# A selective scan's decays issued up to seven units ahead instead of four

## The chip, the cores and the metric

The program runs on one core of a Trainium2 chip. The core has five engines that work side by side: TensorE (PE in the profile, with PEld its weight loads), VectorE (DVE), ScalarE (ACT), GpSimd (POOL) and SyncE (SP), which here issues the DMAs. Each engine takes its instructions strictly in the order in which they were written, and stands still at the first one whose inputs are not there. The metric is the device time of the whole program in microseconds, the median of several runs.

## The reference

The input is 64 images of 96 channels and 28 by 28 pixels. Four layers follow one another:

- layer 0, a convolution block: 1x1 expansion to 576 channels, SiLU, a 5x5 depthwise convolution whose taps are mixed per image, SiLU, a gate, 1x1 projection, residual;
- layer 1, a state-space block: layer norm, projection to 192 channels and a gate `z`, a 3x3 depthwise convolution, SiLU, and then the selective scan in four directions, with 16 states a channel; output norm, gate, projection, and an MLP with GELU;
- layers 2 and 3: layer norm, a Fourier mixing along the 784 positions, and a feed-forward part whose numbers are rounded to 8-bit floats.

What matters here is the scan. Cut from the reference:

```python
dt = jax.nn.softplus(dt)
A = -jnp.exp(A_logs)

def step(hst, inp):
    dt_t, x_t, B_t, C_t = inp
    dA = jnp.exp(dt_t[..., None] * A[None])
    dBx = dt_t[..., None] * B_t[:, :, None, :] * x_t[..., None]
    hst = hst * dA + dBx
    y_t = jnp.einsum('bkdn,bkn->bkd', hst, C_t)
    return (hst, y_t)
```

`dA` is called the decay below. Softplus needs Exp and Ln; the other layers need SiLU and GELU, and those functions lie in other tables of ScalarE than Exp and Ln.

## The kernel before

**Units.** The images go through in 32 pairs. For one pair the scan is cut into 12 blocks (four directions `k`, three tiles `T` of channels), each block into 16 units `n`. A unit is one tile of 128 rows (32 channels by 4 states) and 784 positions. With `j = n % 4` the unit takes the `j`-th group of 32 channels, and with `g = n // 4` the `g`-th group of four states. So the four units of a group share one `pb` (the B row, spread by TensorE into PSUM), and the four groups of a block share the same four tiles of `dt` and of `u = dt * x`, called `dt4` and `u4`.

One unit (`recur`, `decay` and the loop in `run`):

- ACT, `decay`: `da = Exp(A * dt4)`;
- DVE: `pd = pb * u4` (L1045), then the scan `h` over `da` and `pd` (L1050 or, backwards, L1052);
- POOL: `h = h * cs`, with the C row `cs`;
- PE, `collect`, once in four units: sums over the states into `yp`; `keep` copies `yp` out and SP stores it.

**Order.** Nothing is scheduled at run time. `run` walks over all units, one a step, and writes the instructions of each step down in order: the collection of an earlier group, the product and scan of unit `i`, decays of later units, POOL's multiplication for unit `i - 1`, the `pb` of the next group, the loads. `prepare_block` loads the next block's `dt4` and `u4` from DRAM, one tile at each of the steps that the tuples in it name (`at` is `n` of the current block); `fetch_c` loads `cs`.

**Streams.** Between the steps two streams of other work are written: stream `a` (`first_half`) does layer 0 and the front of layer 1 for the next pair, and stream `b` (`second_half`) the rest of the previous pair. Each has one PSUM bank, `bank_a` or `bank_b`: PE fills it, ACT or DVE empties it, and PE waits for that before the next piece. How many pieces stand between two steps is decided by a small planner, `Clocks`, which adds up assumed durations, an ACT table load of 1.28 among them (`activation`), and by how late a stream is. What is left of a stream at the end of a pair is written before the next pair. Stream `a` also writes the `dt` and `u` of the next pair to DRAM (`product`).

**Decays.** `AHEAD = 4`. The decays of the first four units stand before the scan. At step `i`, when the table that ACT holds is Exp's (`act.current == EXP_LN`), or when fewer than four units are decayed, everything up to unit `i + 4` is decayed. Otherwise, with SiLU's or GELU's table in place, the step goes without; the next step then forces the table back, with two decays behind it. The pool `das` has five buffers, so the decay of unit `i + 4` waits until the scan of unit `i - 1` has read its own. The pool `reps` holds five buffers for `dt4` and five for `u4`.

Loads of Exp's table are recorded at line 152 (`preload_act_table_set`), those of the others at line 157.

Of the kernel before, what the change touches and what calls it, by code (L numbers as in the profile page):

```python
# [35 lines left out]
F32 = mybir.dt.float32  # L36
# [10 lines left out]
L = HW * HW  # L47
# [21 lines left out]
EXP_LN = "natural_log_exp_and_others"  # L69
# [1 line left out]
ROWS5, ROWS3 = 16, 14  # L71
BSLOT = 4 * NF

AHEAD = 4

# [112 lines left out]
class Stream:  # L190
# [10 lines left out]
    def after(self, windows, run):  # L201

        self.later.setdefault(self.window + windows, []).append(run)
# [21 lines left out]
class Model:  # L225
# [3 lines left out]
    def __init__(self, ctx, tc, a, out):  # L229
        self.tc, self.nc, self.a, self.out = tc, tc.nc, a, out  # L230
        self.clocks = Clocks()
        self.alone, self.turn = False, 0
        self.act = Act(tc.nc, self.clocks)
        self.vector, self.gpsimd = Timed(tc.nc.vector, self.clocks.vector), Timed(tc.nc.gpsimd, self.clocks.gpsimd)
        self.npairs = a["x"].shape[0] // 2
        pool = lambda name, bufs, **kw: ctx.enter_context(tc.tile_pool(name=name, bufs=bufs, **kw))
        self.cst = pool("cst", 1)
        self.slots = pool("slots", 1)
        self.small = pool("small", 2)
        self.reps = pool("reps", 5)  # L240
        self.das = pool("das", 5)
        self.hs = deque(self.cst.tile([128, L], F32, name=f"h{i}") for i in range(8))
        self.css, self.bss = pool("css", 3), pool("bss", 2)
        self.rows_a = pool("rows_a", 2)
        self.one = pool("one", 1)
        self.ps1 = pool("ps1", 1, space=PSUM)
        dram = lambda name, bufs: pool(name, bufs, space=bass.MemoryType.DRAM)
        self.dr1, self.dr2, self.dr4 = dram("dr1", 1), dram("dr2", 2), dram("dr4", 4)
        self.setup()
# [270 lines left out]
    def first_half(self, p, st):  # L520
        nc, act = self.nc, self.act
        after = lambda n, run: self.a_stream.after(n, run)
        dma = nc.sync.dma_start
# [7 lines left out]
        for i, k in enumerate((k0, k1)):  # L531
            t = k[:, : 10 * C]
# [37 lines left out]
        pool = self.small.tile([C, 2], F32, name="pool")  # L570
# [108 lines left out]
        for t in range(18):  # L679
            n, h = divmod(t, 2)  # L680
            i = order[n]
# [80 lines left out]
        for b in range(2):  # L762
            for h in range(2):
# [7 lines left out]
                v = xs[b][:, cols(h)]  # L771
# [159 lines left out]
        def product(k, T, dt, x):  # L931
            self.gpsimd.tensor_mul(us[0], dt, x)
            dma(st["dt"][k][T], dt)
            after(1, lambda: dma(st["u"][k][T], us[0]))

        def steps(k):

# [44 lines left out]
    def prepare_block(self, u, at):  # L982

        nc, st, k, T = self.nc, u["st"], u["k"], u["T"]
        if at == 1:
            if u["blk"] in (0, 1, 6, 7):
                self.bs[k] = self.bss.tile([C, L], BF16, name="bsl")
                nc.sync.dma_start(self.bs[k], st["b"][k])
        for name, v, when in (("dt4", "dt", (7, 10, 11, 12)), ("u4", "u", (9, 13, 14, 15))):
            if at in when:  # L990
                j = when.index(at)
                t = self.reps.tile([128, L], F32, name=name)
                self.landed[(u["p"], u["blk"], name, j)] = nc.sync.dma_start(
                    t, st[v][k][T][32 * j : 32 * j + 32, None, :].broadcast_to([32, 4, L])
                )
                self.rep[(u["p"], u["blk"], name, j)] = t
# [87 lines left out]

    def run(self):
        nc, act, clocks = self.nc, self.act, self.clocks
        sts = [dict(p=p) for p in range(self.npairs)]
        self.rep, self.cs, self.bs, self.done, self.stored = {}, {}, {}, None, None
        self.multiplied = self.spread_at = 0.0
        self.past, self.landed = deque(), {}  # L1090
        units = [u for st in sts for u in self.scan_state(st["p"], st)]
        per = len(units) // self.npairs

        fresh = lambda i: 0 < i < len(units) and self.key(units[i]) != self.key(units[i - 1])

        def stream(name, p, start=0):
            pieces = self.first_half if name == "a" else self.second_half
            v = Stream(name, clocks, pieces(p, sts[p]), WINDOWS[name] / (per - 2 - start), start)
            setattr(self, name + "_stream", v)
            return v  # L1100

        def advance(streams, until):


            for v in streams:
                v.begin()
            begins = lambda v: max(clocks.pe, clocks.free["ba"[self.turn] if self.alone else v.name])
            while streams:
                streams = [v for v in streams if begins(v) <= until(v)]
                if streams:  # L1110
                    v = min(streams, key=lambda v: begins(v) - CHOICE * late.get(v, 0))
                    if not v.piece():
                        streams.remove(v)

        late = {}

        def finish(streams):
            while any(not v.over for v in streams):
                advance([v for v in streams if not v.over], lambda v: math.inf)


        first, setup = stream("a", 0), Stream("b", clocks, self.setup_second(), 1, 0)
        while not (first.ready and setup.over):
            advance([v for v in (first, setup) if not v.over and not v.ready], lambda v: math.inf)
            self.alone = setup.over
        first.base, first.rate = first.window, 1
        for at in range(16):
            self.prepare_block(units[0], at)
        self.fetch_c(units[0])
        for u in units[:AHEAD]:  # L1130
            self.decay(u)
        decayed = AHEAD
        clocks.dve = max(clocks.dve, clocks.pe)
        self.spread_b(units[0])
        streams = [first]
        for i in range(len(units) + 6):
            u = units[i] if i < len(units) else None
            n = i % per

            if u and n == 0:  # L1140
                self.alone = i // per in (0, self.npairs - 1)
            if i < per and first.over and streams == [first]:
                streams = [stream("a", 1, n)]
            elif u and n == 0 and i > 0:
                streams = [stream("a", i // per + 1, n)] if i // per + 1 < self.npairs else []
            elif u and n == 6 and i // per > 0:
                streams.append(stream("b", i // per - 1, n))
            if i % 4 == 2 and 6 <= i < len(units) + 3:
                self.collect(units[i - 6 : i - 2])
            if u:  # L1150
                self.recur(u)

                if act.current == EXP_LN or decayed < i + AHEAD:
                    for v in units[decayed : i + AHEAD + 1]:
                        self.decay(v)
                    decayed = i + AHEAD + 1
            if 0 < i <= len(units):
                v = units[i - 1]
                clocks.pool = max(clocks.pool, v["scanned"])
                v["users"] = [self.gpsimd.tensor_mul(v["h"], v["h"], self.cs[self.key(v)])]  # L1160
                v["times_c"] = clocks.pool
            if u:
                if fresh(i + 1):
                    self.spread_b(units[i + 1])
                if i + 16 - u["n"] < len(units):
                    self.prepare_block(units[i + 16 - u["n"]], u["n"])
                if u["k"] == 0 and u["n"] == 8:
                    self.x = self.one.tile([128, L], F32, name="xy")
                    nc.sync.dma_start(self.x, u["st"]["x_in"][u["T"]])
            if i + 3 < len(units) and self.key(units[i + 3]) not in self.cs:  # L1170
                self.fetch_c(units[i + 3])
            if i % 4 == 3 and self.done:
                self.keep()
            elif i % 4 == 0 and self.stored:
                nc.sync.dma_start(*self.stored)
                self.stored = None
            if u:

                late.clear(); late.update({v: v.base + (n + 1 - v.start) * v.rate - v.window for v in streams})
                until = clocks.dve + (EARLY if fresh(i + 2) else ROOM)  # L1180
                due = [v for v in streams if not v.over and (v.open or late[v] > -BEFORE)]
                advance(due, lambda v: until + GAIN * late[v] + max(0, late[v] - (per - n) / 4))
                if n == per - 1:
                    finish(streams)
        finish([stream("b", self.npairs - 1)])
# [512 lines left out]
```

## Time and profile before

| | |
|---|---|
| median of 3 runs | 22,441.52 us (22,433.54 to 22,450.66) |
| profiled execution | 22,503.17 us, span 22,501.5 us |
| mean granted TensorE clock in it | 0.832 of full speed |
| ACT: decays `da` (L157) | 6144, mean 940 ns |
| ACT: table loads | 1124, mean 1283 ns |
| DVE: product (L1045), scan (L1050, L1052) | 6144, mean 979 ns; 6144, mean 1786 ns |
| POOL: `h * cs` (L137) | 6144, mean 1856 ns |
| SP: loads of `dt4`, of `u4` (L993) | 1536 and 1536, 392 KB each |

A row of the profile that names a group gives line, engine, operation, what it writes and reads, the count, then the busy time, the mean of one, and the idle time of the engine just before with what ended it. In a timeline a row gives start, duration, engine, line, operation, tiles and count, and in brackets the idle time before it. A line like L157 or L137 is that of a helper, so groups are told apart by their tiles: `da<-dt` is a decay, `pd<-pb,u` the product, `slot` a buffer of stream `b`, `r`, `k`, `t`, `o` and `pad` buffers of stream `a`. An instruction that waits for several things is put down to one of them, not always to the last.

### The profile page before, as it was taken

The numbers are of one execution on the slowest core, as the hardware profiler recorded it, in microseconds if no ns is written. First come the engines' busy times: TensorE is split into PE (matmuls) and PEld (weight loads), VectorE is DVE, ScalarE is ACT, GpSimd is POOL, SyncE is SP. The second block draws the span as 40 slices with busy tenths as digits, with TensorE's granted clock in tenths as the row PEclk, the third lists the DMA queues.
The fourth block names the chain that finished last, engine by engine and source line by source line (L and its number), as shares of the span: only waits on it lengthen the run. The fifth ranks groups of instructions, "written<-read, shape, count | busy, mean of one in ns | idle before, by whom it ended". The sixth has DMA issues, their size and how long they took to land. (4 is left out here: it accounts for less than half of the span.)

```text
span 22501.5 us, 294265 instructions
## 1 busy us (share of the span) xinstructions
PE 17323.6 (77%) x100890; PEld 6770.9 (30%) x100890; DVE 18393.0 (82%) x15290; ACT 13649.8 (61%) x19357; POOL 15987.8 (71%) x9834
## 2 busy tenths in 40 slices
PE   5778777787777777777877777877778777778766
PEld 2233323332323333323323233323233232333222
DVE  2988888888888888888888888888888888888884
ACT  3566666666666666666666666666666666666654
POOL 2777777777777777777777777777777777777774
PEclk8888888888878888888888888888888888888877
DMA  5766666666666666666666666666666666666642
GB/s 155 229 189 197 201 203 187 191 193 200 202 194 187 189 195 198 205 192 192 192 196 200 193 189 197 196 197 200 193 191 190 195 202 193 193 193 190 199 158 63
DMA packets 1764775, 4285.68 MB, mean 190 GB/s; under 512 B 212500, under 2 KB 447084, under 8 KB 1763177
## 3 DMA queue, kind: packets, MB, share of 16 engines
q1 hardware_dynamic: 1763276, 4266.86, 62.0%
q8 instruction: 799, 13.09, 0.2%
q14 instruction: 700, 5.73, 0.1%
HBM read 3207.28 MB, written 882.92 MB: 182 GB/s over the span
## 5 line engine op out<-in xcount | busy, mean ns | idle before, releaser
L137 POOL TENSOR_TENSOR h<-h,cs 128x784 f32<-128x784 f32 x6144 | 11357.7, 1856 | 3875.7 <-DVE h L1050 1175.6
L1045 DVE TENSOR_TENSOR pd<-pb,u 128x784 f32<-128x784 f32 x6144 | 6016.4, 979 | 2346.6 <-PE pb L253 1029.1
L157 ACT ACTIVATE da<-dt,c_A_logs 128x784 f32<-128x784 f32 x6144 | 5661.2, 940 | 2014.4 <-DVE h L1052 865.4
L1052 DVE TENSOR_TENSOR_SCAN h<-da,pd 128x784 f32<-128x784 f32 x3072 | 5487.5, 1786 | 152.9 <-DVE pd L1045 2.8
L1050 DVE TENSOR_TENSOR_SCAN h<-da,pd 128x784 f32<-128x784 f32 x3072 | 5487.4, 1786 | 130.5
L253 PE MATMUL bank_a<-k,t 128*32 128x392 f32 (+1 forms) x37840 | 3984.7, 529 | 204.3 <-ACT pad L157 122.9
L253 PE MATMUL yp<-h,c_gather 128*32 128x512 f32 (+1 forms) x24576 | 3058.3, 595 | 131.3 <-POOL h L137 121.4
L137 POOL TENSOR_TENSOR slot<-slot,slot 96x392 f32<-96x392 f32 (+6 forms) x1700 | 2203.4, 1301 | 1197.3 <-ACT slot L157 988.8
L157 ACT ACTIVATE slot<-bank_b 128x392 f16<-128x392 f32 (+4 forms) x2546 | 1245.4, 489 | 2277.4 <-PE bank_b L253 2235.4
L253 PE MATMUL pb<-bsl,c_sel 96*128 96x512 bf16 (+1 forms) x4096 | 1192.2, 378 | 1320.4 <-DVE pd L1045 1294.1
L253 PEld LDWEIGHTS bank_a<-k,t 128*32 128x32 f32 (+1 forms) x37840 | 1267.2, 116 | 2391.1 <-issue 1894.3
L253 PEld LDWEIGHTS yp<-h,c_gather 128*32 128x32 f32 x24576 | 797.2, 124 | 2472.3 <-issue 2032.4
L253 PE MATMUL bank_b<-slot,c_center 96*128 96x392 f32 x1736 | 955.3, 638 | 396.1 <-DVE slot L137 243.8
L253 PE MATMUL bank_b<-c_fwd,slot 99*96 99x196 f32 (+1 forms) x3968 | 844.7, 359 | 354.1 <-DVE slot L137 254.9
L253 PEld LDWEIGHTS <-c_sel 96*128 96x128 bf16 x4096 | 353.5, 103 | 2469.8 <-issue 1666.9
L157 ACT ACTIVATE o<-bank_a,bn_b,bn_s 128x392 f32<-128x392 f32 x572 | 385.1, 673 | 1113.1 <-PE bank_a L253 1113.1
L157 ACT ACTIVATE slot<-slot 96x786 f32<-96x786 f32 (+5 forms) x1166 | 890.0, 790 | 85.9 <-DMA slot<-in_dt_w 37.6
L253 PEld LDWEIGHTS bank_b<-c_fwd,slot 99*96 99x96 f32 x3968 | 664.9, 175 | 583.4 <-issue 483.1
L157 ACT ACTIVATE slot<-bank_b,c_l_mix 96x393 f32<-96x393 f32 x736 | 446.1, 638 | 632.5 <-PE bank_b L253 418.0
L137 POOL TENSOR_TENSOR k<-k,r 128x784 f32<-128x784 f32 x256 | 472.0, 1844 | 423.1 <-ACT k L157 276.4
L253 PE MATMUL bank_a<-k,cv_diag 96*32 96x392 f32 x4464 | 612.2, 683 | 207.6 <-DMA k<-padded 175.8
L253 PE MATMUL bank_a<-k,k 108*128 108x392 bf16 x744 | 331.2, 445 | 567.5 <-ACT k L157 203.2
(265 smaller groups left out, 20797.5 us busy)
## 6 DMA issues: line engine op xcount, KB each, us to landing
cs<-crow SPq DMA_DIRECT2D x2048, 392.0 KB
dt<-dt SPq DMA_DIRECT2D x1536, 392.0 KB
u<-u SPq DMA_DIRECT2D x1536, 392.0 KB
k<-padded SPq DMA_DIRECT2D x2304, 256.0 KB
padded<-pad SPq DMA_DIRECT2D x384, 592.0 KB
u<-k SPq DMA_DIRECT2D x384, 392.0 KB
k<-padded SPq DMA_DIRECT2D x576, 224.0 KB
out<-o SPq DMA_DIRECT2D x288, 392.0 KB
```

Source lines behind the costliest of these rows:

```text
L137: return run(out, *args, **kw)
L157: return self.nc.scalar.activation(out, in_, func, **kw)
L253: return self.nc.tensor.matmul(out, weights, moving, **kw)
L1045: self.awaited(nc.vector.tensor_mul(pd[:, :L], self.pb[:, :L], self.rep[(u["p"], u["blk"], "u4", u["j"])]), inputs)
L1050: scan = nc.vector.tensor_tensor_scan(h, da, pd[:, :L], 0.0, ALU.mult, ALU.add)
L1052: scan = nc.vector.tensor_tensor_scan(h[:, ::-1], da[:, ::-1], pd[:, L - 1 :: -1], 0.0, ALU.mult, ALU.add)
```

## The change

- `AHEAD` is 7, and a second mark, `LEAST`, is 3. At step `i`, under Exp's table, at most two units are decayed, and none beyond `i + 7`; under another table nothing is decayed until the reserve has come down to three (`decayed <= i + LEAST`), and then two units are, which brings Exp's table back. So the reserve falls for some steps and is filled by one net unit a step. Seven decays stand before the scan instead of four.
- `das` has eight buffers. `dt4` gets a pool of its own, `dts`, with seven buffers; `reps` keeps `u4` alone.
- `dt4` of the next block is loaded at the steps 5, 7, 9 and 10 instead of 7, 10, 11 and 12; `u4` at the same steps as before. An assertion at build time says that the `dt` or `u` read has been written by then.
- The program is built with `dynamic_dma_scratch_size=1024`; the default of the build is 16384 bytes of each partition. The five further tiles of 784 floats need 15,680 bytes a partition.

```diff
-AHEAD = 4
+AHEAD, LEAST = 7, 3
...
         self.reps = pool("reps", 5)
-        self.das = pool("das", 5)
+        self.dts = pool("dts", 7)
+        self.das = pool("das", AHEAD + 1)
...
         def product(k, T, dt, x):
             self.gpsimd.tensor_mul(us[0], dt, x)
             dma(st["dt"][k][T], dt)
-            after(1, lambda: dma(st["u"][k][T], us[0]))
+            st["made"].add(("dt", k, T))
+
+            def second():
+                dma(st["u"][k][T], us[0])
+                st["made"].add(("u", k, T))
+
+            after(1, second)
...
-        for name, v, when in (("dt4", "dt", (7, 10, 11, 12)), ("u4", "u", (9, 13, 14, 15))):
+        for name, v, when in (("dt4", "dt", (5, 7, 9, 10)), ("u4", "u", (9, 13, 14, 15))):
             if at in when:
                 j = when.index(at)
-                t = self.reps.tile([128, L], F32, name=name)
+                assert u["p"] == 0 or (v, k, T) in st["made"]
+                t = (self.dts if v == "dt" else self.reps).tile([128, L], F32, name=name)
...
-                if act.current == EXP_LN or decayed < i + AHEAD:
-                    for v in units[decayed : i + AHEAD + 1]:
+                if act.current == EXP_LN or decayed <= i + LEAST:
+                    for v in units[decayed : min(decayed + 2, i + AHEAD + 1)]:
                         self.decay(v)
-                    decayed = i + AHEAD + 1
+                        decayed += 1
...
-    nc = bacc.Bacc("TRN2", target_bir_lowering=False, num_devices=1)
+    nc = bacc.Bacc("TRN2", target_bir_lowering=False, num_devices=1, dynamic_dma_scratch_size=1024)
```

More of the change, by code (lines that the diff above doesn't have):

```diff
@@ L1086, in run @@
         nc, act, clocks = self.nc, self.act, self.clocks
-        sts = [dict(p=p) for p in range(self.npairs)]
+        sts = [dict(p=p, made=set()) for p in range(self.npairs)]
         self.rep, self.cs, self.bs, self.done, self.stored = {}, {}, {}, None, None
```

## The prediction

> **What bounds the kernel now.** First the page: the span and the busy row.
>
> ```profile
> span 22501.5 us, 294265 instructions
> PE 17323.6 (77%) x100890; PEld 6770.9 (30%) x100890; DVE 18393.0 (82%) x15290; ACT 13649.8 (61%) x19357; POOL 15987.8 (71%) x9834
> ```
>
> VectorE (DVE) is nearest to the span; ScalarE (ACT), where the change works, is busy 61%. So ACT work counts only where DVE waits for it in the end. Second, twelve windows on one pair of images (pair 15, 10586.6 to 11273.3 us), one per block of 16 units; shown are blocks 0, 9, 10, 11 and the sum. Columns after the window: length, then busy PE, PEld, DVE, ACT, POOL.
>
> ```profile
> 10586.60:10647.40 60.80, 34.46 (x125) 11.98 (x124) 46.43 (x38) 40.24 (x61) 44.91 (x28) 0.64 0.66 232
> ...
> 11071.00:11135.60 64.60, 49.30 (x277) 19.04 (x270) 44.23 (x34) 37.04 (x48) 47.20 (x30) 0.71 0.66 198
> 11135.60:11205.30 69.70, 55.52 (x269) 31.83 (x267) 52.04 (x47) 48.90 (x73) 52.83 (x35) 0.85 0.53 178
> 11205.30:11273.30 68.00, 47.28 (x156) 15.55 (x155) 46.53 (x41) 44.76 (x67) 49.11 (x30) 0.64 0.55 183
> sum 686.70, PE 541.98 PEld 212.59 DVE 573.55 ACT 428.41 POOL 501.24; mean PE 45.16 PEld 17.72 DVE 47.80 ACT 35.70 POOL 41.77
> ```
>
> A step is 686.7 / 192 = 3.58 us. DVE idles 686.7 − 573.55 = 113 us a pair: 20.4 + 17.7 + 21.5 us in blocks 9 to 11, 14.4 in block 0, and some 39 in blocks 1 to 8. Third, what ended DVE's waits before its product, L1045, in total, times:
>
> ```profile
>   PE pb L253: 1029.1, 422
>   ACT slot L157: 415.8, 122
>   ACT xy L157: 221.4, 24
>   ACT r L157: 190.8, 53
>   DMA u<-u: 162.7, 21
> ```
>
> The product reads `pb` and `u4`, not ACT's decays. Pairing each of the 6144 products with its decay by order, the decay had ended a median 10.1 us earlier, and only 13 ended less than 1 us before. No decay is late: more reserve by itself buys nothing. The ACT names are other waits of the same instruction; in both stretches below it is `pb` or `u4` that came last.
>
> **The change part by part.**
>
> *Table loads.* ACT's groups, before:
>
> ```profile
> L152 ACT ACT_TABLE_LOAD x562 | 721.0, 1283 | 10.8 <-PEq L1687 0.7
> L157 ACT ACT_TABLE_LOAD x562 | 721.0, 1283 | 10.1
> ```
>
> The changed program's order has 502 + 530 = 1032 loads for 1124. 92 × 1.283 = 118 us of ACT, 2.9 loads or 3.7 us a pair: less than the marks suggest, since other Exp and Ln work already brings the table back often. [...]
>
> Where it can reach DVE, at unit 16 (ACT's timeline, TensorE's, DVE's):
>
> ```profile
> 10641.23 1.28 ACT L152 ACT_TABLE_LOAD   x1
> 10642.52 1.79 ACT L157 ACTIVATE da<-dt,c_A_logs 128x784 f32<-128x784 f32 x2
> 10644.22 0.33 ACT L157 ACTIVATE r<-bank_a 128x128 f32<-128x128 f32 x2
> ```
> ```profile
> 10644.60 2.85 PE L253 MATMUL bank_a<-k,t 128*128 128x384 f32 x8 [0.91 <-ACT r L157]
> 10647.28 0.50 PE L253 MATMUL pb<-bsl,c_sel 96*128 96x512 bf16 x2
> ```
> ```profile
> 10647.97 0.98 DVE L1045 TENSOR_TENSOR pd<-pb,u 128x784 f32<-128x784 f32 x1 [3.50 <-ACT r L157]
> ```
>
> A forced load and two decays, 3.07 us, stand ahead of the eviction `r`; PE loses 0.91 us, then comes `pb`, and DVE waits 3.50 us. In the changed order this load and both decays follow the evictions. Ends 0 and −3.5 us a pair; I take −0.9, PE's own loss, because PE has 2.85 us of matmuls left before `pb` anyway. The other 1.9 loads a pair (2.4 us) end between 0 and −2.4 us; I take −0.5, near zero, since PE's bank waits hide most of ACT (ACT waited 3302 us for `bank_b`, PE 869 for ACT there).
>
> *Decays earlier, two a step.* A decay seven ahead in 8 buffers needs the scan of the unit before this one, the rule that four ahead in 5 had. So the full reserve stops ACT as before (865.4 + 681.3 us behind L1052 and L1050). By the order 3191 of 5700 decays are issued at seven; the other 44% find free buffers, up to 680 us less ACT waiting. But 1429 steps issue two decays for 523, which holds the evictions behind by 0.94 us each, 42 − 15 = 27 us a pair over evictions that mostly have slack. I cost both at 0; the cover is the reserve of `pb` in blocks 1 to 8, and if it is gone the second is in the rival below.
>
> *dt4 earlier; SP's order.* SP, ACT and DVE around the third block, before:
>
> ```profile
> 10673.66 5.64 SPq L494 DMA_DIRECT2D slot<-slot  x8
> ...
> 10681.13 1.47 SPq L1247 DMA_DIRECT2D slot<-z  x3
> 10682.70 2.80 SPq L506 DMA_DIRECT2D k<-padded  x4
> 10686.26 3.17 SPq L993 DMA_DIRECT2D dt<-dt  x3
> ...
> 10695.28 2.54 SPq L506 DMA_DIRECT2D k<-padded  x4
> 10698.03 0.52 SPq L993 DMA_DIRECT2D u<-u  x1
> ```
> ```profile
> 10697.09 0.95 ACT L157 ACTIVATE da<-dt,c_A_logs 128x784 f32<-128x784 f32 x1 [11.20 <-DMA dt<-dt]
> ```
> ```profile
> 10708.74 0.98 DVE L1045 TENSOR_TENSOR pd<-pb,u 128x784 f32<-128x784 f32 x1 [2.34 <-DMA u<-u]
> ```
>
> ACT stops 11.2 us for unit 33's dt4, 10.8 us after its issue behind a burst; then unit 34's u4, issued behind copies that waited for PE, lands too late. In the changed order u4 of units 34 and 35 stand ahead of those four copies: −2.34 us at most, 0 at least; I take −2.0, as the same wait came in most pairs (162.7 us, of which one of 102.7 lies at the start).
>
> ACT's stop stays. Of dt4 for the next block, the third (step 9) and fourth (step 10) are first used two steps later when the reserve is full, 7.2 us; before it was three, 10.7 us. The shortest time from a dt4 issue to its decay in the trace is about 5.7 us, the burst's 10.8: so the wait is 0 to 3.6 us a place. In the third block the fourth dt4 now goes behind the `z` loads: with section 6's sizes, counted from the start of the burst up to the tile itself: before, 980 (`slot`) + 784 (`u`, `cs`) + 1176 (`z`) + 1024 (`k`) + 392 = 4356 KB, landed by 10697, 187 KB a us; now the third dt4 as well, 4748 KB, 2 us later. ACT's release moves from 10697 to about 10699. On DVE: ends 0 and +2.0 there, 0 and +3.6 at the entry of block 9, where the evictions are nearest to DVE's path; I take +0.5 in all, because the reserve itself covers the decays and only the evictions behind them are late. What SP's moved loads pass costs no more: issue is about 0.5 us each, and they are as many.
>
> *Order of the streams.* The planner counts the loads, so pieces move between groups in blocks 1 to 8; from block 10 on (and nearly from 9) PE's order is the same. So 74 of the 113 idle us cannot move by this. Ends for the rest: −39 (all idle of blocks 1 to 8), and +9.3, the longest single wait for `pb`. Nearest is the average over many small moves: I take 0.
>
> *The scratch.* Section 3 of the page lists no software queue and section 6 none but SP's issues, so I cost it at 0; if those shared the scratch, eight issues (5.64 us) doubled would be +5.6 us a pair. [...]
>
> Sum: −0.9 − 0.5 − 2.0 + 0.5 = −2.9 us a pair, × 31 pairs = −90 us. The profiled execution took 22,503 us, 62 above the median; it would be 22,413, and the median 22,441.5 − 90 = 22,350.
>
> **The rivals.**
> *Slower:* the two-step margin. Place: the decays of dt4's third and fourth tile; ACT stands, `bank_a` and `bank_b` are not emptied, `pb` comes late. Price 2.0 + 3.6 us a pair less the 1.4 of the loads: +4.2 × 31 = +130, 22,570. It decides once a dt4 takes over 7.2 us in two places a pair. For: the 10.8 us row. Against: in block 9 ACT runs behind anyway.
> *No change:* DVE's waits are `pb` behind PE's own order; what ACT saves goes into its wait for `bank_b`. 22,441.
> *Larger gain:* the waits at units 16 and 34 go whole and the other loads count: −3.5 − 2.3 − 2.4 = −8.2 × 31 = −254, 22,190. Against: PE has its own work ahead of `pb`.
>
> **How the numbers follow.** ±0.2% (45 us) is about what a measurement can tell from no change. Forecast 0.35 (own range 22,260 to 22,396), larger gain 0.14, no change 0.20, slower 0.31. Faster 0.49. The range 22,200 to 22,590 leaves out about half of the larger gains and the worst of the slower case.
>
> **What would show it.** 1032 loads of 1283 ns; DVE's wait at unit 16 below 3.5 and at unit 34 gone; ACT still stopped for `dt<-dt`, now on the third and fourth tile; blocks 10 and 11 as long as before. Wrong if `da<-dt` waits well over 407 us, or if `pb` is late at new places in blocks 2 to 8.

## The result and the profile after

The changed kernel takes 22,684.8 us (median of 4 runs, 22,660.1 to 22,701.0), the kernel before, beside it, 22,438.8. The ratio is 1.0108, with a 95% interval of 1.009 to 1.0125: 246 us slower. The profiled execution took 22,675.95 us, at the same mean granted TensorE clock of 0.83. The span and the busy row of its page:

```profile
span 22673.0 us, 293585 instructions
PE 17224.7 (76%) x100890; PEld 6734.6 (30%) x100890; DVE 18566.6 (82%) x15290; ACT 13481.0 (59%) x19265; POOL 16003.1 (71%) x9834
```

ACT has 169 us less to do than before (13,649.8) and DVE 174 us more (18,393.0). ACT's groups, the answer to the row of table loads:

```profile
L157 ACT ACTIVATE da<-dt,c_A_logs 128x784 f32<-128x784 f32 x6144 | 5561.9, 939 | 1691.2 <-DMA dt<-dt 912.9 <-DVE h L1058 489.5 <-DVE h L1060 226.5
L157 ACT ACT_TABLE_LOAD x530 | 680.0, 1283 | 9.6
L152 ACT ACT_TABLE_LOAD x502 | 644.1, 1283 | 9.8 <-PEq L1695 0.7
```

1032 loads of 1283 ns: the 118 us are saved. The waits of decays for a scan (`h`) fell from 865.4 + 681.3 to 716.0 us. But the waits for `dt<-dt` rose to 912.9 us. In the kernel before they were 407.4 (in total, times, longest):

```profile
ACT da L157 <- DMA dt<-dt: 407.4, 86, 13.3
```

What ended DVE's waits before its product (now L1053), total and times:

```profile
  PE pb L254: 1312.9, 515
  ACT slot L157: 294.8, 70
  ACT xy L157: 139.8, 15
  ACT r L157: 120.3, 40
  DMA u<-u: 112.4, 5
```

`u<-u` came down from 21 waits to 5, the first of them at the start of the program; `pb` costs 284 us more. Windows on pair 15 of the changed kernel, from each block's first product to the next block's (blocks 0, 1, 2, 9, 10, 11; columns as in the prediction):

```profile
10693.54:10754.17 60.63, 33.81 (x126) 11.37 (x124) 46.44 (x38) 37.11 (x58) 44.79 (x28) 0.66 0.67 233
10754.17:10815.54 61.37, 50.98 (x293) 17.50 (x292) 47.30 (x38) 28.31 (x43) 35.39 (x22) 0.87 0.75 203
10815.54:10867.13 51.59, 45.80 (x322) 14.67 (x320) 48.98 (x42) 28.64 (x39) 37.09 (x22) 0.99 0.58 171
...
11180.99:11246.78 65.79, 50.86 (x288) 18.01 (x288) 45.81 (x36) 36.37 (x51) 51.03 (x34) 0.74 0.69 203
11246.78:11319.75 72.97, 52.38 (x267) 30.02 (x265) 59.09 (x46) 50.89 (x76) 52.46 (x34) 0.86 0.50 164
11319.75:11390.06 70.31, 48.86 (x160) 16.34 (x161) 48.35 (x41) 46.73 (x69) 50.75 (x30) 0.66 0.58 185
```

The same windows of the kernel before, blocks 1 and 2:

```profile
10647.97:10700.37 52.40, 47.49 (x292) 16.85 (x290) 47.46 (x38) 21.79 (x35) 30.95 (x19) 0.93 0.73 181
10700.37:10756.60 56.23, 47.78 (x310) 15.31 (x312) 49.08 (x44) 32.58 (x44) 39.23 (x24) 0.91 0.71 212
```

Block 1 is 9 us longer, with the same DVE work. As means over pairs 2 to 29, in us, with two kernels of the experiments beside them:

| block | 0 | 1 | 2 | 3 | 4 | 5 | 6 | 7 | 8 | 9 | 10 | 11 | sum |
|---|---|---|---|---|---|---|---|---|---|---|---|---|---|
| before | 60.8 | 52.9 | 56.3 | 46.7 | 51.6 | 53.5 | 53.6 | 55.7 | 52.7 | 64.6 | 70.1 | 67.9 | 686.5 |
| changed | 60.4 | **62.5** | 51.3 | 46.4 | 50.6 | 51.8 | 53.0 | 56.4 | 52.9 | 64.2 | 72.5 | 69.5 | 691.5 |
| changed, all `dt4` early (experiment 8) | 60.4 | 51.0 | 50.5 | 46.4 | 49.2 | 52.5 | 52.8 | 56.9 | 53.1 | 65.2 | 71.8 | 68.5 | 678.4 |
| before, four ahead, `dt4` early (experiment 3) | 61.1 | 52.8 | 51.0 | 46.5 | 51.3 | 53.2 | 53.8 | 55.6 | 52.2 | 62.8 | 69.0 | 68.3 | 677.6 |

A pair is 5.0 us longer: 9.6 in block 1, 4.0 in blocks 10 and 11, against 5.0 gained in block 2 and 3.3 in blocks 4 to 6. 32 x 5.0 = 160 of the 171.5 us between the two spans (the profiled execution of before lay 62 us above its median, so the medians are further apart).

**Where block 1 stops.** SP's queue, then ACT, TensorE and DVE of the changed kernel, late in block 1 of pair 15 (start, duration, idle before in brackets):

```profile
10780.62 5.66 SPq L495 DMA_DIRECT2D slot<-slot  x8
10786.38 3.47 SPq L507 DMA_DIRECT2D k<-padded  x4
10789.90 0.53 SPq L1001 DMA_DIRECT2D dt<-dt  x1
...
10793.83 0.53 SPq L1001 DMA_DIRECT2D dt<-dt  x1
```
```profile
10786.18 0.95 ACT L157 ACTIVATE da<-dt,c_A_logs 128x784 f32<-128x784 f32 x1 [0.24 <-DVE h L1060]
10795.86 0.95 ACT L157 ACTIVATE da<-dt,c_A_logs 128x784 f32<-128x784 f32 x1 [8.74 <-DMA dt<-dt]
10802.58 0.95 ACT L157 ACTIVATE da<-dt,c_A_logs 128x784 f32<-128x784 f32 x1 [5.77 <-DMA dt<-dt]
10803.44 0.66 ACT L157 ACTIVATE o<-bank_a,bn_b,bn_s 128x392 f32<-128x392 f32 x1
```
```profile
10791.98 2.88 PE L254 MATMUL bank_a<-k,t 128*32 128x392 f32 x32
10795.23 0.93 PE L254 MATMUL bank_b<-slot,c_cen_d 128*128 128x392 f32 x2 [0.36 <-DVE slot L137]
10796.08 0.92 PE L254 MATMUL bank_b<-slot,neg_d 64*128 64x392 f32 x2
10804.15 1.68 PE L254 MATMUL bank_a<-r,c_exp_w 96*128 96x392 f32 x2 [7.14 <-ACT o L157]
10805.75 1.57 PE L254 MATMUL bank_b<-slot,neg_d 128*64 128x392 f32 x2
```
```profile
10799.32 1.79 DVE L1060 TENSOR_TENSOR_SCAN h<-da,pd 128x784 f32<-128x784 f32 x1
10811.85 0.62 DVE L137 SCALAR_TENSOR_TENSOR slot<-bank_b,c_on,slot 128x392 f32<-128x392 f32 x1 [10.74 <-PE bank_b L254]
```

Read it from the top. Unit 25's product started at 10783.34; the third `dt4` tile, written at that step, is issued only at 10789.90, because twelve issues worth 9.1 us stand before it in SP's queue. ACT comes to its decay at 10787.12, before the load is even issued, and stands 8.74 us (1.89 of them it would have waited for a free buffer, as experiment 6 shows); the fourth tile costs 5.77 more. Directly behind the second stop stands the eviction `o`. TensorE has filled `bank_a` by 10794.86 and has 1.8 us of other work; then its next instruction wants `bank_a` empty. It stands 7.14 us, and behind it stand the `bank_b` matmuls that DVE waits for: it loses 10.74 us, with the decays of units 31 to 34 all there. TensorE and then ACT in the kernel before, at the same place of its pair 15:

```profile
10692.33 2.89 PE L253 MATMUL bank_a<-k,t 128*32 128x392 f32 x32
10695.04 1.50 PE L253 MATMUL yp<-h,c_gather 128*32 128x512 f32 x16
10696.47 0.87 PE L253 MATMUL bank_b<-slot,neg_d 128*64 128x392 f32 x2
...
10700.02 0.82 PE L253 MATMUL bank_a<-r,c_exp_w 96*128 96x392 f32 x2
```
```profile
10698.46 0.66 ACT L157 ACTIVATE o<-bank_a,bn_b,bn_s 128x392 f32<-128x392 f32 x1
```

There ACT stood 11.20 us for a `dt4` too (the row stands in the prediction), and `o` followed only at 10698.46; but between the last matmul into `bank_a` and the next one TensorE had 5 us of other work, and the stop was over before it wanted the bank. Counted from the block's first product, the stop ended at 49.1 us there and the second stop at 48.4 us in the changed kernel, so it was not a later end of the stop that cost the time.

### The profile page after: what moved, and what is told of

Read it like the earlier page. It is cut to its first block, busy times and chain, and to the rows that moved or that the text cites. A ratio compares the mean times of both kernels' runs of the same rounds, so it can differ in the third digit from the quotient of the medians.

```text
span 22673.0 us, 293585 instructions
## 1 busy us (share of the span) xinstructions
PE 17224.7 (76%) x100890; PEld 6734.6 (30%) x100890; DVE 18566.6 (82%) x15290; ACT 13481.0 (59%) x19265; POOL 16003.1 (71%) x9834
## 5 line engine op out<-in xcount | busy, mean ns | idle before, releaser
L1053 DVE TENSOR_TENSOR pd<-pb,u 128x784 f32<-128x784 f32 x6144 | 6015.5, 979 | 2325.4 <-PE pb L254 1312.9
L157 ACT ACTIVATE da<-dt,c_A_logs 128x784 f32<-128x784 f32 x6144 | 5561.9, 939 | 1691.2 <-DMA dt<-dt 912.9
L254 PE MATMUL bank_a<-k,t 128*32 128x392 f32 (+1 forms) x37840 | 3924.2, 524 | 154.1 <-ACT pad L157 108.6
L157 ACT ACTIVATE slot<-bank_b 128x392 f16<-128x392 f32 (+4 forms) x2546 | 1245.2, 489 | 2674.6 <-PE bank_b L254 2634.9
L254 PE MATMUL bank_b<-c_fwd,slot 99*96 99x196 f32 (+1 forms) x3968 | 795.2, 344 | 355.2 <-DVE slot L137 284.2
L254 PE MATMUL bank_a<-r,c_exp_w 96*64 96x392 f32 (+1 forms) x1218 | 610.2, 672 | 478.7 <-ACT o L157 323.7
L157 ACT ACTIVATE o<-bank_a,bn_b,bn_s 128x392 f32<-128x392 f32 x572 | 385.8, 674 | 978.4 <-PE bank_a L254 976.1
L157 ACT ACTIVATE slot<-slot 96x786 f32<-96x786 f32 (+5 forms) x1166 | 890.2, 790 | 87.1 <-DMA slot<-in_dt_w 38.3
L254 PE MATMUL bank_b<-slot,slot 96*128 96x392 f32 x1488 | 688.6, 568 | 184.6 <-ACT slot L157 122.6
```

Of the source, the lines that this page charges most:

```text
L157: return self.nc.scalar.activation(out, in_, func, **kw)
L254: return self.nc.tensor.matmul(out, weights, moving, **kw)
L1053: self.awaited(nc.vector.tensor_mul(pd[:, :L], self.pb[:, :L], self.rep[(u["p"], u["blk"], "u4", u["j"])]), inputs)
```

## The experiments

Ratios are to the kernel before, run on the same chip in between, with 95% intervals; its medians there were 22,449.9 to 22,468.4 us.

**1. Is it the longer DVE operation?** The added DVE time is one group, the maximum of two SBUF tiles (last section). Its work is folded into the operation before it, in the changed kernel and in the kernel before (the folded form leaves out the absolute value).

```diff
-                self.vector.tensor_tensor(zi, zi, zr, ALU.max)
...
+                self.vector.scalar_tensor_tensor(zi, pi, di, zr, ALU.mult, ALU.max)
```

> The changed kernel, with DVE's 96x393 `max` of two SBUF tiles (attention, `middle`) replaced by a scalar_tensor_tensor one window earlier that reads the PSUM bank and one SBUF tile. It leaves out the absolute value of that input, so that it is still one instruction; ACT's Abs stays, its result unused. Theory 1 (DVE's max stands behind runs of GpSimd work: in the trace its third and fourth instances in the last layer of each pair take a mean of 3.12 and 5.08 us, in the kernel before 0.67 and 1.15): the time falls by about 31 x (8.21 - 1.82) = 198 us, from 22,685 to some 22,490, and no DVE instruction of the mixing takes over 1 us. Theory 2 (the loss is ACT's stop for dt4, and DVE's wait at unit 30, 11.95 us a pair): it stays within 40 us of 22,685.

> The same replacement in the kernel before (it leaves out the same absolute value). Theory 1: its max instances took 4.5 us a pair beyond... their sum over eight is 5.77 us where eight undisturbed ones are 4.31, so about 45 us to gain and 22,395 to 22,440. Theory 2 says nothing of it: 22,440. [...]

Measured: 22,718.1 us, 1.0109 (1.0096 to 1.0122), and 22,485.2, 1.0005 (0.9996 to 1.0014). DVE's busy time of the changed kernel fell to 18,380.5 us, all that had been added, and the time stayed. Block 10 went from 72.5 to 71.5 us, block 11 from 69.5 to 71.2: in that stretch DVE waits anyway. The long operation is not the cause.

**2. Three `dt4` tiles earlier; the scratch alone.** `dt4` of the changed kernel at other steps; and the kernel before with the small scratch.

```diff
-        for name, v, when in (("dt4", "dt", (5, 7, 9, 10)), ("u4", "u", (9, 13, 14, 15))):
+        for name, v, when in (("dt4", "dt", (3, 4, 5, 10)), ("u4", "u", (9, 13, 14, 15))):
```

> The changed kernel with the loads of dt4 at the steps 3, 4, 5 and 10 instead of 5, 7, 9 and 10. Theory 2: ACT's stop for dt4 (913 us in the changed kernel, 407 before) falls by more than half, DVE's wait at unit 30 falls from 11.95 us to 5 or less, and the time by 100 to 200 us, to 22,490 to 22,590. Theory 1: those waits may shrink, yet the time stays within 60 us of 22,685 as long as the two max instances keep their 3 and 5 us.

> The kernel before with the scratch of 1024 bytes alone. [...] Were the scratch the cause, it would take 22,685.

Measured: 22,581.4 us, 1.0047 (1.0035 to 1.0059); the waits for `dt<-dt` are 644.8 us, and the fourth tile of the third block, the one not moved, now stops ACT for 13.2 us at unit 35. Block 1 is still 61.9 us, with DVE's wait of 11.3 us at unit 30. So the time came as Theory 2 had it, but not in its way: the waits for `dt<-dt` fell by 29%, not by half, and the wait at unit 30 stayed. The scratch: 22,462.9, 0.9995 (0.9986 to 1.0003), nothing.

**3. `dt4` early without the marks.** The kernel before with its reserve of four, a pool of eight `dt4` buffers, all four loads early, and the small scratch. ACT and TensorE have the order of the kernel before.

```diff
+        self.dts = pool("dts", 8)
...
-        for name, v, when in (("dt4", "dt", (7, 10, 11, 12)), ("u4", "u", (9, 13, 14, 15))):
+        for name, v, when in (("dt4", "dt", (3, 4, 5, 6)), ("u4", "u", (9, 13, 14, 15))):
...
-                t = self.reps.tile([128, L], F32, name=name)
+                t = (self.dts if v == "dt" else self.reps).tile([128, L], F32, name=name)
```

> The kernel before (four ahead, its own rule), with dt4 in a pool of eight buffers, loaded at the steps 3, 4, 5 and 6, and the scratch of 1024 bytes. The order of TensorE and ScalarE is word for word that of before. Theory A (ACT's stop for dt4 delays the evictions behind it and so PE and DVE): the 11.4 us stop at unit 33 goes, DVE's waits at units 29 to 35 (9 us a pair) fall to 3 or less, and the time falls by 100 to 200 us, to 22,270 to 22,370. Theory C (DVE's time in blocks 1 and 2 is set by the order of the streams' pieces on PE, and ACT's stop is covered): within 40 us of 22,450.

Measured: **22,230.1 us, 0.99 (0.9887 to 0.9914)**, the fastest kernel of all (with the first of experiment 7, within noise). The waits for `dt<-dt` are 12.0 us. Most of the gain is block 2 (56.3 to 51.0), behind the old stop for unit 33's `dt4`.

**4. Late tiles without the marks.** The changed kernel with the rule of before: always up to seven ahead under Exp's table, forced when one is missing. 1124 loads; but for two groups, TensorE's order is that of before.

```diff
-                if act.current == EXP_LN or decayed <= i + LEAST:
-                    for v in units[decayed : min(decayed + 2, i + AHEAD + 1)]:
+                if act.current == EXP_LN or decayed < i + AHEAD:
+                    for v in units[decayed : i + AHEAD + 1]:
```

> The changed kernel with the rule of before: seven ahead at all times, refilled at once under Exp's table, forced as soon as one is missing. 1124 table loads, and PE's order is that of before but for two groups of units; dt4 at the steps 5, 7, 9 and 10, as in the change. Theory A: the reserve is always full, so dt4's third and fourth tile stop ACT as in the change or more (over 900 us in all), and the time is 22,600 to 22,750. Theory B (a part of the loss is the refill of the reserve in block 10, where ACT is late): block 10 returns from 72.5 to about 70 us, since there is nothing to refill. Theory C: with PE's old order the time is 22,440 to 22,500.

Measured: 22,404.0 us, 0.9983 (0.9974 to 0.9992). ACT's chain of waits in this kernel:

```profile
ACT da L157 <- DMA dt<-dt: 917.4, 295, 16.5
```

That is as much as in the changed kernel, 12.6 us a pair of it at unit 35, behind the same burst; yet block 1 takes 53.1 us, 0.2 more than before. Late tiles alone do not cost the time of block 1. The forecasts of the time by Theories A and C both missed; that of Theory B for block 10 came, 69.3 us.

**5. Six ahead with the marks, `dt4` early; no refill late.** First the marks at 6 and 3 with `dt4` as in 3; then the same with no more than four ahead from unit 144 on.

```diff
-AHEAD, LEAST = 7, 3
+AHEAD, LEAST = 6, 3
...
-                    for v in units[decayed : min(decayed + 2, i + AHEAD + 1)]:
+                    for v in units[decayed : min(decayed + 2, i + (AHEAD if n < 144 else 4) + 1)]:
```

> The changed kernel with the two marks 6 and 3, dt4 in eight buffers, loaded at the steps 3, 4, 5 and 6; 1094 table loads. Theory A: no stop for dt4 is left (under 100 us in all), and what the fewer loads gave in blocks 3 to 6 stays: 22,300 to 22,430. Theory C: the pieces are ordered anew, so 22,500 to 22,600 in spite of it, with a long wait for `bank_b` in block 1 as in the change.

> As the run before, but from unit 144 of a pair on the reserve is not filled beyond four. Theory B: blocks 10 and 11 take 1 to 3 us a pair less than in the run before, which is 30 to 90 us. Theories A and C alone: the same as the run before within 30 us.

Measured: 22,280.1 us, 0.993 (0.9917 to 0.9942), and 22,543.3, 1.0048 (1.0034 to 1.0061). The second was to win and lost 263 us: block 9 rose from 59.6 to 69.1 us, DVE's wait at unit 152 from 4.58 to 13.64. The cap also changes what the planner writes in that stretch, so it says nothing clean on the refill; that the moved pieces are what cost the 263 us is likely, but not shown.

**6. One tile.** From the kernel of 2 (three tiles early, fourth at step 10) only the fourth tile of the third block is moved, to step 6. The order of TensorE's and ACT's instructions is that of the changed kernel.

```diff
-        for name, v, when in (("dt4", "dt", (3, 4, 5, 10)), ("u4", "u", (9, 13, 14, 15))):
+        for name, v, when in (("dt4", "dt", (3, 4, 5, 6 if u["blk"] == 2 else 10)), ("u4", "u", (9, 13, 14, 15))):
```

> The changed kernel with dt4 loaded at the steps 3, 4, 5 and 10, and at 3, 4, 5 and 6 for the third block alone; the orders of TensorE and ScalarE are word for word those of the changed kernel. Theory D (the loss is ACT's stop for dt4 in block 1, behind which the two marks have put the eviction `o` that PE needs next; neither the stop nor the new order costs it alone): ACT's stops at units 34 and 35 go, DVE's wait at unit 30 falls from 12 us to 3 or less, block 1 falls from 62 to some 54 us, and the time to 22,280 to 22,380. Theory C (the new order of the pieces by itself): as the run with the early loads, about 22,580, with the wait at unit 30 in its place.

Measured: 22,276.6 us, **0.9911 (0.9896 to 0.9927)**. One 392 KB load a pair, four steps earlier, is worth 305 us (1.0047 to 0.9911), and block 1 takes 51.0 us. Its window in pair 15, then ACT, TensorE and DVE at the same instructions:

```profile
10572.88:10623.84 50.96, 46.97 (x296) 16.84 (x294) 47.29 (x39) 28.41 (x43) 35.46 (x21) 1.00 0.75 189
```
```profile
10607.72 0.95 ACT L157 ACTIVATE da<-dt,c_A_logs 128x784 f32<-128x784 f32 x1 [1.89 <-DVE h L1060]
10610.56 0.95 ACT L157 ACTIVATE da<-dt,c_A_logs 128x784 f32<-128x784 f32 x1 [1.89 <-DVE h L1060]
10613.65 0.68 ACT L157 ACTIVATE o<-bank_a,bn_b,bn_s 128x392 f32<-128x392 f32 x1 [2.14 <-PE bank_a L254]
```
```profile
10610.69 2.89 PE L254 MATMUL bank_a<-k,t 128*32 128x392 f32 x32
...
10615.64 0.93 PE L254 MATMUL bank_a<-r,c_exp_w 96*128 96x392 f32 x2
10617.16 0.87 PE L254 MATMUL bank_b<-slot,neg_d 128*64 128x392 f32 x2 [0.59 <-DVE slot L137]
```
```profile
10620.47 0.62 DVE L137 SCALAR_TENSOR_TENSOR slot<-bank_b,c_on,slot 128x392 f32<-128x392 f32 x1 [0.66 <-PE bank_b L254]
```

The decays wait 1.89 us for a buffer, `o` waits for TensorE, not the reverse, and DVE's 10.74 us are 0.66.

**7. Six ahead without marks; the change's steps without the reserve.** The marks of 5 replaced by the rule of before, `dt4` early; and the kernel before, four ahead, with the change's seven `dts` buffers, steps (5, 7, 9, 10) and scratch.

> Six ahead at all times by the rule of before, dt4 in eight buffers at the steps 3, 4, 5 and 6; PE's order is nearly that of before. If the reserve itself is worth nothing, as no decay is late with four: the same as four ahead with the same loads, 22,230 within 40 us. If a reserve does help: 22,190 or less.

> The kernel before with only the change's loads of dt4 (pool of seven, steps 5, 7, 9 and 10) and the scratch. With four ahead the first use comes 7, 6, 5 and 5 steps after the load instead of 5, 3, 3 and 3. Theory A and D: the stop at unit 33 goes in part or whole (its tile is now ahead of the burst), and the time falls to 22,230 to 22,330; so the loads that the change moves are a gain by themselves, taken back by the seven ahead. Theory C: 22,440.

Measured: 22,235.5 us, 0.9894 (0.9881 to 0.9908), and 22,384.2, 0.9963 (0.995 to 0.9975). Six ahead and four ahead (experiment 3) are the same within noise: the reserve itself is worth nothing. The change's own `dt4` steps are a gain of 0.4% with a reserve of four; `da<-dt` waits only 36.3 us there, since a tile loaded at step 9 is wanted at step 14 and not at 11. Its time missed the forecast of Theories A and D: with the stops as good as gone it still takes 154 us more than experiment 3. So the steps 3, 4, 5 and 6, with eight buffers for seven, take away more than ACT's stops; what else they take away stays open.

**8. Every tile early.** As 6, with the two other places at which ACT still stopped, units 83 and 131.

```diff
-        for name, v, when in (("dt4", "dt", (3, 4, 5, 6 if u["blk"] == 2 else 10)), ("u4", "u", (9, 13, 14, 15))):
+        for name, v, when in (("dt4", "dt", (3, 4, 5, 6 if u["blk"] in (2, 8) else 8 if u["blk"] == 5 else 10)), ("u4", "u", (9, 13, 14, 15))):
```

> The changed kernel with dt4 loaded at steps 3, 4, 5 and 10, and the fourth tile of three blocks earlier: step 6 for the third block (as in the run that took away the stop of block 1), now also step 6 for the ninth block and step 8 for the sixth. In the run with the third block alone early, ScalarE still stopped 263.5 us for dt4, 6.15 us a pair at unit 131 and 2.18 us at unit 83. Theory D (a late dt4 costs only where an eviction that TensorE needs stands directly behind the stop): these two stops go, da<-dt under 60 us, and the time stays within 40 us of 22,277; the two marks are then worth nothing beside the rule of before with early loads (22,230 and 22,235). Rival (every late dt4 reaches VectorE): 8.3 us a pair comes back, 31 x 8.3 = 258 us, near 22,020, which would be below the rule of before with early loads, so that the marks would be worth some 200 us.

Measured: 22,277.9 us, 0.9919 (0.9904 to 0.9933). ACT's chain of waits:

```profile
ACT da L157 <- DMA dt<-dt: 17.8, 6, 11.6
```

The stops of 6.15 and 2.18 us a pair are gone, and the time is that of experiment 6 within noise (0.9919 and 0.9911, on two chips). So the stop in block 1 cost some 305 us and those in blocks 5 and 8 nothing that can be measured.

**What follows.** In block 1, where the changed kernel loses its time, neither half costs it. The stop alone does not (4: 917 us of stops in all, block 1 takes 53.1 us), the new order of the streams alone does not (6: the same order, 51.0); the two together make 62.5, for 52.9 before. Over the whole kernel late tiles are not free without the marks either: experiment 4 is at 0.9983 and the first of experiment 7, without late tiles and one unit fewer ahead, at 0.9894, 6.7 us a pair less. Where those go was not followed up; with the marks the late tiles cost twice that, 13.2 us a pair (691.5 and 678.3). The table shows what the marks do once nothing is late, against four ahead with its own early loads (experiment 3): blocks 0 to 6 gain 6.9 us a pair, blocks 7 to 11 lose 7.6. Part of the loss stands where the reserve is refilled (ACT spends 17.4 us on decays in block 10, before 14.9), but that this is its cause was not shown: the run that should have shown it moved the streams as well. In its favour, without the marks block 10 takes 69.3 us in experiment 4, with TensorE's order there nearly that of the changed kernel; against it, 68.9 us with the marks of 6 and 3 in experiment 5.

## Why the prediction was wrong

It said 22,350 us, faster at 0.49, within 22,200 to 22,590; measured were 22,684.8, beyond the range on the slower side.

- *Table loads*: 1032 of 1283 ns, as counted, with next to no idle time ahead of them: 9.6 us before the 530 at L157 and 9.8 us before the 502 at L152.
- *Unit 16* (−0.9, ends 0 and −3.5): the mean wait fell from 3.56 to 3.26 us. The load and the decays did leave, but TensorE was the limit. In pair 15, with no decay in ACT's way, `r` waits 2.68 and 2.94 us for TensorE, and DVE 3.19. So the rival of the larger gain fell for the reason given against it.
- *Unit 34* (−2.0): right in kind and too small. The mean wait went from 3.02 us to none, and block 2 is 5.0 shorter.
- *Other loads* (−0.5): blocks 4 to 6 are 3.3 us a pair shorter. How much of that comes from the loads and how much from the moved pieces cannot be told.
- *`dt4` earlier* (+0.5, ends +2.0 and +3.6): **this is the step that failed**, together with *order of the streams* at 0: for the +0.5 us a pair of both, block 1 became 9.6 us longer. The place and the stop were named; three things in the working were not right. First, the margin of "two steps, 7.2 us" was counted from the step, where the load is written, and not from where SP reaches it: the twelve issues before it, 9.1 us of SP's time, used it up. I had costed these issues only by the KB they move. So the third tile stopped ACT as well, 7.7 us a pair, beside the fourth's 7.1. A wait of 0 to 3.6 us a place had been allowed for, and in the third block the fourth tile alone was reckoned with; the total went to 912.9 us. Second, the price was the shift of the stop, on the ground that ACT had stopped there before and the reserve covers the decays. The shift itself was no loss: in pair 15 the release came 0.7 us earlier in the block than before, not 2 later. But what had made it harmless was 5 us of other TensorE work between two uses of `bank_a`, and the edit on the marks moves such pieces. I priced the stop and the order each alone and added them; in block 1 they cost 9.6 us a pair together and nothing apart. Third, nothing stood for the 2.87 us that TensorE lost behind its stop, at a granted clock of 0.50 (last section).
- *The slower rival* (22,570): its mechanism is the one that came, with its place. Its price of 5.6 us a pair was ACT's lateness; the price that counts is TensorE's and DVE's, 13.2 us a pair between the changed kernel and that of experiment 6 (691.5 and 678.3). "Against: in block 9 ACT runs behind anyway" looked at the wrong block.
- *Blocks 10 and 11 as before*: wrong, 2.4 and 1.6 us longer, although TensorE's order is that of before there.
- *Scratch* (0): right: with 1024 bytes alone the kernel before takes 22,462.9 us, 0.9995. The run shows the time, not what uses the scratch.
- *What would make it wrong* was named: `da<-dt` well over 407 us. The profile of after shows it at once; which stop of it matters it shows only in the timeline of four engines.

## What to carry to other kernels

A stop on an in-order engine has no fixed price: in block 1 its price was set by what stood directly behind it and by how much other work the waiting engine had before it wanted that. So when an edit moves both a load and the order around it, follow the stop through the queues in the new order, and count a load's margin from where the issuing queue reaches it, with every issue before it, not from where it is written. Here the cheap part of the change, loads moved up into buffers of their own, was worth 0.4% at the change's steps and 1.0% at earlier ones (experiments 7 and 3), and the reserve that they were to serve nothing.

## What the runs showed of the hardware

**TensorE after a stop.** In the changed kernel `bank_a<-r,c_exp_w` starts 49.98 us after its block's first product, in the kernel of experiment 6 42.76: 7.22 later. DVE's operation behind it starts 57.68 and 47.59 us after: 10.09 later. The other 2.87 us are the four groups between, 1.57 us each for 0.87. Windows of the changed kernel before, in and after the stop (the column behind the busy times is the granted clock):

```profile
10780.00:10796.00 16.00, 14.13 (x134) 4.88 (x126) 15.66 (x13) 3.74 (x6) 9.29 (x5) 1.00 0.84 201
10796.00:10804.00 8.00, 1.00 (x3) 0.29 (x2) 5.04 (x5) 2.23 (x4) 1.84 (x1) 0.70 1.04 329
10804.00:10812.00 8.00, 7.85 (x14) 1.85 (x18) 0.15 (x1) 5.62 (x9) 4.66 (x4) 0.50 1.00 317
```

The granted clock is 0.50 for the 8 us after a stop of 7.14 us; at the same instructions of experiment 6, without the stop, it stays 1.00. In windows of 1 us it is 1.00 up to 10799, 0.61 in the next and then 0.50, so the fall comes at about 10799.2, 2.2 us after TensorE fell idle; it is 0.85 in the window from 10816 and 1.00 in the next, so the full clock comes only at about 10816.3, after 12.1 us of almost unbroken matmuls. Here a stop that made TensorE 7.2 us late made DVE 10.1 us late. What sets the granted clock is not shown.

**A maximum of two SBUF tiles on VectorE, while GpSimd works.** The maximum of experiment 1 in the changed kernel, one line of its tile's view (shortest, median and longest of 256, ns), and DVE and POOL in block 10 of pair 15:

```profile
L137 DVE TENSOR_TENSOR slot<-slot x256: 537/540/6247, 1328.6 to 22616.9; 96x393 f32<-96x393 f32 x128
```
```profile
11287.94 5.55 DVE L137 TENSOR_TENSOR slot<-slot 96x393 f32<-96x393 f32 x1
```
```profile
11285.71 1.97 POOL L137 TENSOR_TENSOR slot<-slot 96x393 f32<-96x393 f32 x2
11287.64 1.84 POOL L137 TENSOR_TENSOR h<-h,cs 128x784 f32<-128x784 f32 x1
11289.44 1.84 POOL L137 TENSOR_TENSOR k<-t,r 128x784 f32<-128x784 f32 x1
11291.23 1.84 POOL L137 TENSOR_TENSOR h<-h,cs 128x784 f32<-128x784 f32 x1
11293.57 1.97 POOL L137 TENSOR_TENSOR slot<-slot 96x393 f32<-96x393 f32 x2 [0.50 <-DVE slot L137]
```

An operation of 0.54 us at the median takes 5.55. It starts at 11287.94, while POOL works, stands through the rest of POOL's operation and two more, and ends at 11293.49, in the 0.50 us for which POOL pauses, itself waiting for a `slot` of DVE. At the place before it in the same pair (11278.10, 3.32 us) it ended at 11281.42 without such a pause: POOL went from one operation straight to the next at 11280.95. At these two places in block 10 it took 3.1 and 5.1 us on average, and 0.67 and 1.15 in the kernel before; in pair 15 of that one 0.54 and 0.88 (11163.86 and 11174.12), also while POOL worked (2.31 us from 11162.83, 2.17 from 11173.56). So a working POOL alone does not make it long, and what does is not shown. All 256 of them took 368.6 us for 184.4 before, DVE as a whole 174 more, and taking it out gave nothing (experiment 1): busy time that only replaces a wait.
